# Two of three contraction parts of the context projections by Strassen's seven products, in a perceiver block on one core

## Chip, core and metric

The kernel runs on one core of a Trainium2 chip. It is timed as the device microseconds of one execution; the time before is the median of three runs, 1639.78 us (1639.32 to 1644.37). Everything is float32. The engines are TensorE (PE, matmuls; its weight loads are shown as PEld), VectorE (DVE), ScalarE (ACT), GpSimd (POOL) and SyncE (SP), which here issues all transfers. Each has its own in-order queue; they wait for each other through semaphores.

## What is computed

A block of three layers: cross attention of 32 batches of 64 tokens (width 512) to a context of 512 tokens (width 384), self attention with rotary angles, and a feed-forward layer for the better half of the tokens. Each is added to x. Cut to what the change touches:

```python
# x: (32, 64, 512); ctx_768: (32, 512, 384); the mask is all true
def _L0_xattn_ref(x, context, context_mask, Wq, Wk, Wv, Wo):      # 16 heads of 32
    q = (x @ Wq)...          # Wq: (512, 512)
    k = (context @ Wk)...    # Wk, Wv: (384, 512)
    v = (context @ Wv)...
    scores = einsum('bhid,bhjd->bhij', q, k) * scale
    attn = softmax(where(context_mask, scores, max_neg), axis=-1)
    out = einsum('bhij,bhjd->bhid', attn, v)
    return out.reshape(B, N, 512) @ Wo
...
x = x + _L0_xattn_ref(_layernorm(x), ctx_768, mask_BxS2_bf1, ...)
x = x + _L0_attn_ref(_layernorm(x), ...)
x = x + _L0_ffn_ref(_layernorm(x), ...)
```

Per batch, keys and values are two products of (512 x 384) by (384 x 512): the largest piece of arithmetic in the block.

## The kernel before, in words

**Stages.** Stage A is the cross attention, stage B the self attention, then comes the feed-forward layer. Stage A is one loop over 66 steps s (line 519); b = s // 2 is the batch and cp = s % 2 says which half of its heads is worked on. One step is called a half here.

**One half, in PE's order.** PE's instructions stand in the order in which the program writes them (`tc.manual_schedule`, line 135). The other engines' orders are made by a scheduler. A half does this:

- `score_burst` (line 188): scores of the half's 8 heads into four PSUM banks sc0 to sc3, 16 records.
- `attend` and `weighted` (lines 232, 501): the weighted sums of the half that was scored two halves ago, into bank po.
- `softmax_a` (line 203): for each of the four banks a reduction on DVE (line 208, writes sm and the minimum mn), the exponential on ACT (line 214, writes pr and its sum), the reciprocal on DVE (line 216), and on POOL the scaling of pr (line 217).
- Four rounds r = 0 to 3. Each has `flip` (line 221: four PE transposes of one pr tile of the half before into the bank pt, and a copy out of it, on DVE for even r, on ACT for odd r) and one `kv_piece` (line 145) for the next batch: in a cp = 0 half the four pieces of the keys, in a cp = 1 half the four pieces of the values. A piece is three matmuls of 512 columns, one for each 128 of the contraction of 384, into a bank "mm", and one copy to SBUF (ACT for keys, DVE for values).
- In every fourth half, `project` (line 246) in round 1: the output projection of a tile of 128 tokens, the addition to x and the statistics of the next layer norm. In cp = 0 halves, as long as a group of four tiles is still to come, round 3 ends with a piece of the next queries (`query_tile` or `query_chunk`).

**Banks.** PSUM has eight: mm twice, pt once, po once, sc0 to sc3. A bank with one buffer is written again only when its reader is done.

**Transfers.** `load_ctx(b)` brings the transposed context (768 KB) and the mask row of batch b into buffers of which there are two; it is called with `kv_start` (line 137) one batch ahead, at the beginning of a cp = 0 half. `kv_start` makes the mask tile mb on POOL. The weights of stage B (awq, awk, awv, awo) are loaded at the start, behind x (lines 130 to 133, awq first).

**The end of stage A.** In the last batch there is no next batch to project; stage B's first tiles (`early`) take the place of the pieces. From there on nothing of the change is in the program, apart from the place of three weight tiles.

Of the kernel before, what the change touches and what calls it, by code (L numbers as in the profile page):

```python
# [7 lines left out]
F32 = mybir.dt.float32  # L8
U8 = mybir.dt.uint8
AF = mybir.ActivationFunctionType  # L10
ALU = mybir.AluOpType
# [3 lines left out]
P = 128  # L15
NB, S, D = 32, 64, 512
M, DC = 512, 384
# [5 lines left out]
NCC = DC // P  # L23
# [17 lines left out]
def perceiver_block(  # L41
# [3 lines left out]
    nc = tc.nc  # L45
# [4 lines left out]
    wbpool = ctx.enter_context(tc.tile_pool(name="wb", bufs=1))  # L50
# [4 lines left out]
    def chunked(w):  # L55
        return w.rearrange("(c p) f -> p c f", p=P)

    def load(pool, w, tag):
        k, f = w.shape
        t = pool.tile([P, k // P, f], F32, tag=tag, name=tag)  # L60
        nc.sync.dma_start(t, chunked(w))
        return t

    def row2k(tag, bufs, name, shape=(P, D)):
        return work.tile(list(shape), F32, tag=tag, name=name, bufs=bufs)
# [3 lines left out]
    def bank(tag, name, shape=(P, 512)):  # L69
        return ps.tile(list(shape), F32, tag=tag, name=name, bufs=2 if tag == "mm" else 1)  # L70
# [33 lines left out]
    wa = only_a.enter_context(tc.tile_pool(name="wa", bufs=1, side="right"))  # L104
    kvp = only_a.enter_context(tc.tile_pool(name="kv", bufs=2, side="right"))

    def load_ctx(b):
        t = kvp.tile([P, NCC, M], F32, tag="ctxT", name=f"ctxT{b}")
        nc.sync.dma_start(t, chunked(ctxT[b]))
        m8 = kvp.tile([P, M], U8, tag="m8", name=f"m8_{b}")  # L110
        nc.sync.dma_start(m8, mask[b : b + 1, :].to_broadcast([P, M]))
        return t, m8
# [6 lines left out]
    wk = load(wa, xWk, "xWk")  # L119
    ctx0 = load_ctx(0)  # L120
    wv = load(wa, xWv, "xWv")
# [6 lines left out]
    wo = load(wa, xWo, "xWo")  # L128
    xs += [load_x(t) for t in range(GT, NT)]
    awq = load(wbpool, aWq, "aWq")  # L130
    awk = load(wbpool, aWk, "aWk")
    awv = load(wbpool, aWv, "aWv")
    awo = load(wbpool, aWo, "aWo")

    tc_order = ctx.enter_context(tc.manual_schedule(engines={mybir.EngineType.PE}))

    def kv_start(b, loaded):
        cT, m8 = loaded
        mb = kvp.tile([P, M], F32, tag="mb", name=f"mb{b}")
        nc.gpsimd.tensor_scalar(mb, m8, -BIG, BIG, ALU.mult, ALU.add)  # L140
        kT = kvp.tile([P, NC, M], F32, tag="kT", name=f"kT{b}")
        v = kvp.tile([P, NKC, D], F32, tag="v", name=f"v{b}")
        return dict(b=b, cT=cT, mb=mb, kT=kT, v=v)

    def kv_piece(kv, n):

        p = bank("mm", f"kv{kv['b']}_{n}")
        i = n % 4
        cols = slice(i * P, (i + 1) * P)
        for d in range(NCC):  # L150
            if n < 4:
                lhsT, rhs = wk[:, d, cols], kv["cT"][:, d, :]
            else:
                lhsT, rhs = kv["cT"][:, d, cols], wv[:, d, :]
            nc.tensor.matmul(p, lhsT, rhs, start=(d == 0), stop=(d == NCC - 1))  # L155
        if n < 4:
            nc.scalar.copy(kv["kT"][:, i, :], p)  # L157
        else:
            nc.vector.tensor_copy(kv["v"][:, i, :], p)  # L159

    def query_group(g):

        for t in range(g * GT, (g + 1) * GT):
            ln_stats(0, t)
        ln_rstd(0, g * GT, GT)
        return dict(
            g=g, xnT=work.tile([P, NC, GT * P], F32, tag="xnT", name=f"xnT_a{g}"),
            qT=work.tile([P, NC, GT * P], F32, tag="qT", name=f"qT_a{g}", bufs=2),
        )
# [33 lines left out]
    def softmax_a(kv, pss, cp):  # L203
        b, prs = kv["b"], []
        for r in range(4):
            sm = row2k("sm", NSM, f"sm{b}_{cp}_{r}")
            mn = small.tile([P, 1], F32, tag="mn", name=f"mn{b}_{cp}_{r}")
            nc.vector.tensor_tensor_reduce(  # L208
                out=sm, in0=pss[r], in1=kv["mb"], scale=1.0, scalar=3.4e38,
                op0=ALU.add, op1=ALU.min, accum_out=mn,  # L210
            )
            pr = row2k("pr", NPR, f"pr{b}_{cp}_{r}")
            su = small.tile([P, 1], F32, tag="su", name=f"su{b}_{cp}_{r}")
            nc.scalar.activation(pr, sm, AF.Exp, bias=mn, scale=-1.0, accum_out=su)  # L214
            ri = small.tile([P, 1], F32, tag="ri", name=f"ri{b}_{cp}_{r}")
            nc.vector.reciprocal(ri, su)  # L216
            nc.gpsimd.tensor_scalar(pr, pr, ri, None, ALU.mult)  # L217
            prs.append(pr)
        return prs

# [215 lines left out]
    def tile_steps(t):  # L436


        live = {}

        def last(n):
            return t - n if 0 <= t - n < NT else None

        here, back, done = last(0), last(1), last(2)
        ahead = t + 1 if t + 1 < NT else None
        if here is not None:
            heads_first(here, 0)
            heads_first(here, 1)
            yield 0.9
        if back is not None:  # L450
            pTs = [flip_b(back, 0, probs[back][0])]
        if ahead is not None:
            norm_b(ahead)
        if back is not None:
            pTs.append(flip_b(back, 1, probs[back][1]))
        yield 1.3
        if here is not None:
            probs[here] = [softmax_b(here, 0)]
        if done is not None:
            live = choose(done)  # L460
        if ahead is not None:
            roped(project_b(ahead, awq, "q"), 0)
            yield 4.1
        if back is not None:
            oT = weighted_b(back, pTs)
        if here is not None:
            probs[here].append(softmax_b(here, 1))
        yield 2.0
        if ahead is not None:
            roped(project_b(ahead, awk, "k"), 1)  # L470
            yield 3.4
        if back is not None:
            project_y(back, oT)
            yield 3.4
        if done is not None:
            gather(done, *live)
        if ahead is not None:
            nc.scalar.copy(slot("xv", 2 + ahead % 2), project_b(ahead, awv, "v"))
            yield 3.4
# [3 lines left out]
    def stage_b(first, last):  # L483
        for t in range(first, last):
            yield from tile_steps(t)


    kv = kv_start(0, ctx0)
    for n in range(8):
        kv_piece(kv, n)  # L490
    group = query_group(0)
    for j in range(GT):
        query_tile(group, j)
    for c in range(NC):
        query_chunk(group, c)
    nxt = kv_start(1, ctx1)

    halves = []
# [18 lines left out]
    ready = None  # L517
    early = None
    for s in range(2 * NB + 2):
        b, cp = s // 2, s % 2  # L520
        if b < NB:
            if s and cp == 0:
                kv = nxt
                nxt = kv_start(b + 1, load_ctx(b + 1)) if b + 1 < NB else None
            pss = score_burst(kv, group["qT"], cp)
        if s >= 2:
            ready = attend()
        flips = halves[0] if halves else None
        if b < NB:
            half = dict(id=f"{b}_{cp}", kv=kv, cp=cp, pTs=[])  # L530
            half["prs"] = softmax_a(kv, pss, cp)
            halves.append(half)
        g, at = divmod(b, 2 * GT)
        if s == 2 * GT * 2 * g and g + 1 < NT // GT and b < NB:
            coming = query_group(g + 1)
        if b < NB and nxt is None and early is None:
            buf["xv"] = work.tile([P, 4, D], F32, tag="xnT", name="xv_b")
            buf["rope"] = work.tile([P, 4, D], F32, tag="wq", name="rope_b")
            buf["qk"] = work.tile([P, 4, D], F32, tag="qT", name="qk_b", bufs=2)
            early = stage_b(-1, 2)  # L540
        more = b < NB and g + 1 < NT // GT
        for r in range(4):
            if flips is not None:
                flip(flips, r)
            if b < NB and nxt is not None:
                kv_piece(nxt, 4 * cp + r)
            elif early is not None:
                spent = 0.0
                while spent < 2.2:
                    took = next(early, None)  # L550
                    if took is None:
                        break
                    spent += took
            if ready is not None and r == 1:
                project(*ready)
                ready = None
            if more and cp == 0 and r == 3:
                if at < GT:
                    query_tile(coming, at)
                else:  # L560
                    query_chunk(coming, at - GT)
        if more and at == 2 * GT - 1 and cp:
            group = coming
# [79 lines left out]
    for fc in range(NFC):  # L643
        tag, bufs = W2_HOME[fc]
# [80 lines left out]
```

## Time and profile before

| | us |
|---|---|
| median of three runs | 1639.78 |
| the profiled execution | 1639.23 |
| its span, first to last instruction | 1637.4 |
| from the start to the first score burst | 47.93 |
| from there to the first score burst of the last batch (62 halves) | 986.62 |
| the last batch's two halves and what follows, to 1110 us | 75.45 |
| stage B's rest and the feed-forward layer | 527.40 |

A half without `project` and without a query piece lasts 14.37 us (1002.39 to 1016.76). In it DVE runs for 3.7 us of reductions, four reciprocals and two flip copies, ACT four exponentials of 0.72 us with 0.19 us to read their sums, POOL four scalings of 1.55 us.

How to read the lines: a group's row has the source line, engine, operation, output <- inputs by the program's names, the shape, the count, then busy us and mean ns of one, and the idle time of the engine just ahead of these instructions with what ended it. A matmul's duration holds its pipeline's fill and drain, so that records that follow each other overlap; what one costs in a stream is the distance from one start to the next. A float32 matmul shows as two records. A row of a timeline has the start, the duration, and in brackets the idle time before it.

### The profile page before, as it was taken

What the parts mean: (1) busy time and instruction counts of PE and PEld (TensorE: products, weight loads), DVE (VectorE), ACT (ScalarE), POOL (GpSimd) and SP (SyncE); (2) the same over time, 40 slices, a digit from 0 to 9 for tenths busy, and PEclk for the clock granted to TensorE, in tenths of its full rate; (3) what the DMA queues carried; (4) which work ended last, traced back from release to release, by engine and by line L of the source; (5) the groups of instructions that cost most, each with busy time, mean ns of one, the idle gap of its engine ahead of it and who ended that gap; (6) DMA issues with size and microseconds to landing.
All of it is one profiled execution on the core that took longest, in us unless ns stands there. A gap on an engine that the chain in (4) does not pass through costs nothing. (4 is left out here: it accounts for less than half of the span.)

```text
span 1637.4 us, 28162 instructions
## 1 busy us (share of the span) xinstructions
PE 1599.7 (98%) x11584; PEld 800.8 (49%) x11584; DVE 683.3 (42%) x1725; ACT 456.5 (28%) x1012; POOL 549.0 (34%) x440
## 2 busy tenths in 40 slices
PE   7999999999999999999999999889999998999998
PEld 3455444554444454544444454445555555444443
DVE  3333434443434343434343343447777777101001
ACT  1343332333323333333233333221222222210100
POOL 0434343434433434434344444433333333000000
PEclk9999999999999999999999999999999999999999
DMA  9100100010001000100010010002000002001001
GB/s 348 41 22 23 42 22 22 24 41 22 23 23 41 22 22 24 41 22 22 23 41 22 23 46 1 1 3 109 1 1 2 1 8 74 24 0 39 13 13 39
DMA packets 29520, 54.58 MB, mean 33 GB/s; under 512 B 2128, under 2 KB 6224, under 8 KB 28880
## 3 DMA queue, kind: packets, MB, share of 16 engines
q1 hardware_dynamic: 29392, 52.77, 9.8%
q8 instruction: 92, 1.51, 0.4%
q14 instruction: 36, 0.29, 0.1%
HBM read 48.57 MB, written 4.19 MB: 32 GB/s over the span
## 5 line engine op out<-in xcount | busy, mean ns | idle before, releaser
L217 POOL TENSOR_SCALAR pr<-pr,ri 128x512 f32<-128x512 f32 x256 | 396.4, 1563 | 535.7 <-DVE ri L216 529.5
L155 PE MATMUL kv<-ctxT,xWk 128*128 128x512 f32 x768 | 351.9, 596 | 7.7 <-DMA ctxT<-in_ctxT 7.7
L155 PE MATMUL kv<-xWv,ctxT 128*128 128x512 f32 x768 | 350.3, 593 | 0.0
L214 ACT ACTIVATE pr<-sm,mn 128x512 f32<-128x512 f32 x256 | 183.7, 718 | 285.6 <-DVE mn L208 220.5
L208 DVE CUSTOM_DVE_ANT_0 sm<-sc,mb 128x512 f32<-128x512 f32 x256 | 171.7, 689 | 87.7 <-PE sc L197 87.7
L155 PEld LDWEIGHTS kv<-ctxT,xWk 128*128 128x128 f32 x768 | 137.2, 191 | 135.0 <-issue 133.9
L155 PEld LDWEIGHTS kv<-xWv,ctxT 128*128 128x128 f32 x768 | 136.2, 190 | 124.3 <-issue 124.1
L101 PEld LDWEIGHTS pt<-cst,pr 128*128 128x128 f32 x1024 | 117.7, 141 | 125.3 <-issue 73.3
L101 PE MATMUL pt<-cst,pr 128*128 128x128 f32 x1024 | 158.9, 278 | 6.6 <-DVE rope_b L288 3.1
L159 DVE COPY v<-kv 128x512 f32<-128x512 f32 x128 | 88.4, 691 | 159.7 <-PE kv L155 159.5
L157 ACT COPY kT<-kv 128x512 f32<-128x512 f32 x128 | 74.8, 585 | 205.9 <-PE kv L155 205.9
L227 ACT COPY pT<-pt 128x512 f32<-128x512 f32 x128 | 73.8, 577 | 203.4 <-PE pt L101 203.4
L611 PE MATMUL ups<-W,hT 128*128 128x512 f32 x256 | 111.8, 595 | 0.0
L229 DVE COPY pT<-pt 128x512 f32<-128x512 f32 x128 | 87.7, 685 | 56.5 <-PE pt L101 56.5
L599 PE MATMUL hps<-selT,W 128*128 128x512 f32 x256 | 110.7, 593 | 0.0
L216 DVE RECIPROCAL ri<-su 128x1 f32<-128x1 f32 x256 | 40.8, 159 | 109.0 <-ACT pr L214 95.4
L338 POOL TENSOR_TENSOR pr_b<-pr_b,ri_b 128x512 f32<-128x512 f32 x32 | 33.4, 1043 | 155.5 <-DVE ri_b L337 146.1
L240 PEld LDWEIGHTS po<-pT,v 128*32 128x32 f32 x4096 | 60.1, 110 | 51.2 <-issue 51.2
L618 DVE TENSOR_TENSOR up<-ups,b_bc 128x512 f32<-128x512 f32 x8 | 5.5, 691 | 176.6 <-PE ups L611 176.6
L611 PEld LDWEIGHTS ups<-W,hT 128*128 128x128 f32 x256 | 48.1, 190 | 62.9 <-issue 62.9
L599 PEld LDWEIGHTS hps<-selT,W 128*128 128x128 f32 x256 | 48.4, 190 | 60.5 <-issue 60.5
L197 PE MATMUL sc<-kT,qT_a 32*64 32x512 f32 x1024 | 71.3, 613 | 0.0
(94 smaller groups left out, 1484.1 us busy)
## 6 DMA issues: line engine op xcount, KB each, us to landing
ctxT<-in_ctxT SPq DMA_DIRECT2D x32, 768.0 KB, 4.8
x<-in_x SPq DMA_DIRECT2D x16, 256.0 KB, 8.9
W<-in_W SPq DMA_DIRECT2D x1, 4096.0 KB, 12.6
W<-in_W SPq DMA_DIRECT2D x16, 256.0 KB, 3.2
out<-o SPq DMA_DIRECT2D x16, 256.0 KB, 2.0
m<-in_mask SPq DMA_DIRECT2D x32, 64.0 KB, 2.8
wq<-in_xWq SPq DMA_DIRECT2D x1, 1024.0 KB, 10.1
xWo<-in_xWo SPq DMA_DIRECT2D x1, 1024.0 KB, 10.4
```

The source lines that it names most:

```text
L101: nc.tensor.transpose(into[:, c, :], src[:, c * P : (c + 1) * P], ident)
L155: nc.tensor.matmul(p, lhsT, rhs, start=(d == 0), stop=(d == NCC - 1))
L157: nc.scalar.copy(kv["kT"][:, i, :], p)
L159: nc.vector.tensor_copy(kv["v"][:, i, :], p)
L197: nc.tensor.matmul(pss[r][S * i : S * (i + 1), :], qT[rows, 2 * cp + i, at : at + S], kv["kT"][rows, 2 * cp + i, :], start=True, stop=True,)
L208: nc.vector.tensor_tensor_reduce(out=sm, in0=pss[r], in1=kv["mb"], scale=1.0, scalar=3.4e38, op0=ALU.add, op1=ALU.min, accum_out=mn,)
L214: nc.scalar.activation(pr, sm, AF.Exp, bias=mn, scale=-1.0, accum_out=su)
L217: nc.gpsimd.tensor_scalar(pr, pr, ri, None, ALU.mult)
L227: nc.scalar.copy(pT, p)
L229: nc.vector.tensor_copy(pT, p)
L599: nc.tensor.matmul(p, w1[:, d, fc * P : (fc + 1) * P], late["selT"][n][:, d, :], start=(d == 0), stop=(d == NC - 1),)
L611: nc.tensor.matmul(p, hTs[n, fc // 4][:, fc % 4, j * P : (j + 1) * P], w2[fc], start=(fc == 0), stop=(fc == NFC - 1),)
```

## The change

Keys and values are each a product with a contraction of 384 = 3 x 128. For the first two parts of 128, the product of a 2 x 2 grid of blocks by a 2 x 2 grid of blocks is made by Strassen's seven products in place of eight; the blocks are 128 (contraction) by 256. The third part keeps its number of columns, as eight matmuls of 256; its terms are accumulated into the banks of the seven products ("lo" and "hi" with "both", "first" or "second", where "both" is the sum of the two halves of the context and serves two of the four result blocks together).

- `weight_sums` makes, once, five sums or differences of weight blocks and one negation, for Wk on DVE and for Wv on POOL.
- `kv_start` makes, for each batch, three DVE instructions of sums and differences of context blocks into cs (512, 256 and 768 elements a partition).
- `kv_steps` is a generator of seven steps for each of keys and values. Its matmuls have 256 columns; steps 1 to 3 have two each and open the banks pb, pa and pc, and each bank is copied out by ACT and then, in steps 4 to 6, accumulated into further, without being cleared. Steps 4 to 7 have four matmuls each. ACT makes five copies, POOL four additions or subtractions in SBUF, DVE two additions of a bank to an SBUF block.
- pc lies in the bank sc0, the fourth bank "d" again in "mm".
- In the four rounds of a half, rounds 0 to 2 take two steps and round 3 takes one. `project` moves from round 1 to the end of round 3 in the halves that have such steps.
- `kv_start` and `load_ctx` are called a half earlier, for batch b + 2, at cp = 1.
- The tiles of awk, awv and awo are used for the sums until the last batch; the three loads move from the start to there.
- The scaling of pr gets a second operation (times 1.0).

```diff
-    awk = load(wbpool, aWk, "aWk")
-    awv = load(wbpool, aWv, "aWv")
-    awo = load(wbpool, aWo, "aWo")
...
+    HALFW = M // 2
+    spare = wbpool.tile([P, 8 * HALFW], F32, tag="aWk", name="spare")
+    wkx = spare[:, 0 : 3 * HALFW].rearrange("p (i f) -> p i f", i=3)
+    held = spare[:, 3 * HALFW : 7 * HALFW].rearrange("p (i f) -> p i f", i=2)
+    wvx = wa.tile([P, 3, HALFW], F32, tag="wvx", name="wvx")
+
+    def weight_sums(w, x, engine):
+        a11, a21 = w[:, 0, 0:HALFW], w[:, 0, HALFW:M]
+        a12, a22 = w[:, 1, 0:HALFW], w[:, 1, HALFW:M]
+        engine.tensor_tensor(x[:, 0, :], a11, a22, ALU.add)
+        engine.tensor_tensor(x[:, 1, :], a21, a22, ALU.add)
+        engine.tensor_tensor(x[:, 2, :], a11, a12, ALU.add)
+        engine.tensor_tensor(a21, a21, a11, ALU.subtract)
+        engine.tensor_tensor(a12, a12, a22, ALU.subtract)
+        engine.tensor_scalar(a11, a11, -1.0, 1.0, ALU.mult, ALU.mult)
...
+    wks = weight_sums(wk, wkx, nc.vector)
+    wvs = weight_sums(wv, wvx, nc.gpsimd)
 
     def kv_start(b, loaded):
         cT, m8 = loaded
+        cs = wbpool.tile([P, 6, HALFW], F32, tag=("aWv", "aWo")[b % 2], name=f"cs{b}")
+        nc.vector.tensor_tensor(
+            cs[:, 3:5, :].rearrange("p i k -> p (i k)"), cT[:, 1, :], cT[:, 0, :], ALU.subtract
+        )
+        nc.vector.tensor_tensor(cs[:, 5, :], cT[:, 0, 0:HALFW], cT[:, 1, HALFW:M], ALU.add)
+        nc.vector.tensor_tensor(
+            cs[:, 0:3, :], cT[:, :, 0:HALFW], cT[:, :, HALFW:M], ALU.add
+        )
...
-    def kv_piece(kv, n):
...
+    def kv_steps(kv, part):
+        w, c, b = (wks, wvs)[part], kv["c"], kv["b"]
+
+        def product(p, wn, cn, start=False, stop=False):
+            for j in range(2):
+                cols = slice(j * P, (j + 1) * P)
+                lhsT, rhs = (c[cn][:, cols], w[wn]) if part else (w[wn][:, cols], c[cn])
+                nc.tensor.matmul(
+                    p[:, j, :], lhsT, rhs, start=start and j == 0, stop=stop,
+                    skip_group_check=True,
+                )
...
+        pb = open_bank("mm", "b")
+        product(pb, "m3", "m3", start=True)
+        nc.scalar.copy(c11, pb)
+        yield
+        pa = open_bank("mm", "a")
+        product(pa, "m4", "m4", start=True)
+        nc.scalar.copy(c22, pa)
+        yield
+        pc = open_bank("sc0", "c")
+        product(pc, "m1", "m1", start=True)
+        nc.scalar.copy(x1, pc)
+        nc.gpsimd.tensor_tensor(c11, c11, c22, ALU.add)
+        nc.gpsimd.tensor_tensor(c22, c11, x1, ALU.add)
+        yield
+        product(pb, "m5", "m5")
+        product(pb, "lo", "second", stop=True)
+        nc.scalar.copy(c12, pb)
+        nc.gpsimd.tensor_tensor(c11, c11, c12, ALU.subtract)
+        yield
+        product(pa, "m2", "m2")
+        product(pa, "hi", "first", stop=True)
+        nc.scalar.copy(c21, pa)
+        nc.gpsimd.tensor_tensor(c22, c22, c21, ALU.subtract)
+        yield
+        product(pc, "m7", "m7")
+        product(pc, "lo", "both", stop=True)
+        nc.vector.tensor_tensor(c11, pc, c11, ALU.add)
+        yield
+        pd = open_bank("mm", "d")
+        product(pd, "m6", "m6", start=True)
+        product(pd, "hi", "both", stop=True)
+        nc.vector.tensor_tensor(c22, pd, c22, ALU.add)
+        yield
...
-            nc.gpsimd.tensor_scalar(pr, pr, ri, None, ALU.mult)
+            nc.gpsimd.tensor_scalar(pr, pr, ri, 1.0, ALU.mult, ALU.mult)
...
             if s and cp == 0:
-                kv = nxt
-                nxt = kv_start(b + 1, load_ctx(b + 1)) if b + 1 < NB else None
+                kv, nxt = nxt, after
...
             halves.append(half)
+            if cp:
+                after = kv_start(b + 2, load_ctx(b + 2)) if b + 2 < NB else None
+            if nxt is not None:
+                steps = kv_steps(nxt, cp)
...
+            awk = load(wbpool, aWk, "aWk")
+            awv = load(wbpool, aWv, "aWv")
+            awo = load(wbpool, aWo, "aWo")
             early = stage_b(-1, 2)
...
             if b < NB and nxt is not None:
-                kv_piece(nxt, 4 * cp + r)
+                next(steps)
+                if r < 3:
+                    next(steps)
...
-            if ready is not None and r == 1:
+            if ready is not None and r == (3 if b < NB and nxt is not None else 1):
                 project(*ready)
                 ready = None
```

More of the change, by code (lines that the diff above doesn't have):

```diff
@@ L130, in perceiver_block @@
     awq = load(wbpool, aWq, "aWq")
-    awk = load(wbpool, aWk, "aWk")
-    awv = load(wbpool, aWv, "aWv")
-    awo = load(wbpool, aWo, "aWo")
     tc_order = ctx.enter_context(tc.manual_schedule(engines={mybir.EngineType.PE}))
+    HALFW = M // 2
[12 more added lines that the diff above has]
+        engine.tensor_scalar(a11, a11, -1.0, 1.0, ALU.mult, ALU.mult)
+        return {
+            "m1": x[:, 0, :], "m2": x[:, 1, :], "m3": a11, "m4": a22, "m5": x[:, 2, :],
+            "m6": a21, "m7": a12, "lo": w[:, 2, 0:HALFW], "hi": w[:, 2, HALFW:M],
+        }
+    wks = weight_sums(wk, wkx, nc.vector)
+    wvs = weight_sums(wv, wvx, nc.gpsimd)
     def kv_start(b, loaded):
         cT, m8 = loaded
+        cs = wbpool.tile([P, 6, HALFW], F32, tag=("aWv", "aWo")[b % 2], name=f"cs{b}")
[6 more added lines that the diff above has]
+        )
         mb = kvp.tile([P, M], F32, tag="mb", name=f"mb{b}")
@@ L142, in kv_start @@
         v = kvp.tile([P, NKC, D], F32, tag="v", name=f"v{b}")
-        return dict(b=b, cT=cT, mb=mb, kT=kT, v=v)
-    def kv_piece(kv, n):
[L147 to L159, printed above, removed]
+        c = {
+            "m1": cs[:, 5, :], "m2": cT[:, 0, 0:HALFW], "m3": cs[:, 4, :], "m4": cs[:, 3, :],
+            "m5": cT[:, 1, HALFW:M], "m6": cs[:, 0, :], "m7": cs[:, 1, :],
+            "first": cT[:, 2, 0:HALFW], "second": cT[:, 2, HALFW:M], "both": cs[:, 2, :],
+        }
@@ new lines, in kv_start, with home, open_bank @@
+        return dict(b=b, c=c, mb=mb, kT=kT, v=v)
+    def kv_steps(kv, part):
[8 more added lines that the diff above has]
+                )
+        def home(f, k):
+            if part:
+                return kv["v"][:, 2 * k : 2 * k + 2, f * HALFW : (f + 1) * HALFW]
+            return kv["kT"][:, 2 * f : 2 * f + 2, k * HALFW : (k + 1) * HALFW]
+        def open_bank(tag, n):
+            return bank(tag, f"kv{b}_{part}_{n}", (P, 2, HALFW))
+        c11, c12, c21, c22 = home(0, 0), home(0, 1), home(1, 0), home(1, 1)
+        x1 = held[:, part, :].rearrange("p (j k) -> p j k", j=2)
+        pb = open_bank("mm", "b")
[31 more added lines that the diff above has]
+        yield
@@ L488, in perceiver_block @@
     kv = kv_start(0, ctx0)
-    for n in range(8):
-        kv_piece(kv, n)
+    for part in range(2):
+        for _ in kv_steps(kv, part):
+            pass
     group = query_group(0)
```

## The prediction

> **What bounds the kernel now.** I read the page first, then the same engines by stretch, then one period in order of time.
>
> ```profile
> PE 1599.7 (98%) x11584; PEld 800.8 (49%) x11584; DVE 683.3 (42%) x1725; ACT 456.5 (28%) x1012; POOL 549.0 (34%) x440
> ...
> L155 PE MATMUL kv<-ctxT,xWk 128*128 128x512 f32 x768 | 351.9, 596 | 7.7 <-DMA ctxT<-in_ctxT 7.7
> L155 PE MATMUL kv<-xWv,ctxT 128*128 128x512 f32 x768 | 350.3, 593 | 0.0
> ...
> L101 PE MATMUL pt<-cst,pr 128*128 128x128 f32 x1024 | 158.9, 278 | 6.6 <-DVE rope_b L288 3.1
> ```
>
> TensorE (PE) is busy 98% of the span. The projection that is changed, L155, is 1536 of its records: 32 batches x 2 parts x 12 matmuls, each matmul shown as two records. The transposes of line 101 lost 6.6 us in all, so the vector engines are never felt. By stretches of time, the steady part of stage A is full:
>
> ```profile
> 47.93:1034.55 986.62, 984.68 (x7561) 485.86 (x7560) 396.90 (x1092) 342.34 (x784) 411.44 (x295) 1.00 0.09 26
> ```
>
> Columns: length, then busy time of PE, PEld, DVE, ACT, POOL, then the granted clock (1.00). In 986.62 us PE is busy 984.68. That says that PE work removed is time removed, but only until another engine stands just behind. So I look at one half-batch ("half") in order of time, PE and then VectorE (DVE):
>
> ```profile
> 1002.39 1.11 PE L197 MATMUL sc<-kT,qT_a 32*64 32x512 f32 x16
> 1003.44 1.10 PE L240 MATMUL po<-pT,v 128*32 128x64 f32 x64
> 1004.47 0.66 PE L101 MATMUL pt<-cst,pr 128*128 128x128 f32 x4
> 1004.96 2.74 PE L155 MATMUL kv<-ctxT,xWk 128*128 128x512 f32 x6
> 1007.59 0.63 PE L101 MATMUL pt<-cst,pr 128*128 128x128 f32 x4
> ...
> 1016.76 1.11 PE L197 MATMUL sc<-kT,qT_a 32*64 32x512 f32 x16
> ```
>
> ```profile
> 1002.50 0.69 DVE L159 COPY v<-kv 128x512 f32<-128x512 f32 x1 [2.33 <-PE kv L155]
> 1003.57 0.69 DVE L208 CUSTOM_DVE_ANT_0 sm<-sc,mb 128x512 f32<-128x512 f32 x1 [0.37 <-PE sc L197]
> 1004.18 0.69 DVE L208 CUSTOM_DVE_ANT_0 sm<-sc,mb 128x512 f32<-128x512 f32 x1
> ...
> 1005.30 0.16 DVE L216 RECIPROCAL ri<-su 128x1 f32<-128x1 f32 x1 [0.42 <-ACT pr L214]
> 1005.44 0.69 DVE L208 CUSTOM_DVE_ANT_0 sm<-sc,mb 128x512 f32<-128x512 f32 x1
> ...
> 1006.14 0.69 DVE L208 CUSTOM_DVE_ANT_0 sm<-sc,mb 128x512 f32<-128x512 f32 x1
> ...
> 1006.76 0.69 DVE L229 COPY pT<-pt 128x512 f32<-128x512 f32 x1
> ```
>
> Measure all from the score burst (1002.39 = 0). The half lasts 14.37. The first flip starts at 2.08, the first projection piece at 2.57, the second flip at 5.20. There is one "pt" bank, so the second flip must wait until DVE has copied the first flip out. That copy stands behind four softmax reductions in DVE's queue, runs from 4.37 and ends at 5.06. **The margin before DVE holds PE is 5.20 - 5.06 = 0.14 us.** That is the number on which this change turns.
>
> **The change part by part.**
>
> *Matmul columns.* Per part 12 matmuls of 512 columns become 22 of 256: 24 records to 44. Price: six 512-column records and the flip behind them repeat every 3.01-3.02 us (601.62 to 604.63 elsewhere in the timeline); four 128-column records take 0.44 of it, so a 512-column one takes 0.429 and a 128-column one 0.107 to 0.11. No record has 256 columns. From below, in proportion: 0.2145. From above, the 64-column records of L428, the nearest ordinary matmuls with full weights (eight in 1.00 us, 0.125 each): the line from there to 0.429 gives 0.255. I take 0.2145, because the 128-column records lie on the proportional line. The weight loads last 0.19 and fit under it. So 24 x 0.429 - 44 x 0.2145 = 0.86 us less PE work per half, 64 x 0.86 = 55 us in all.
>
> [...]
>
> *Where the columns go.* Between the first and the second flip stood one piece, 6 x 512 = 3072 columns. Now the first two steps stand there, 8 records x 256 = 2048. Behind the second flip stood 18 x 512; now 12 + 16 + 8 = 36 records x 256, the same 9216. **The whole saving lies ahead of the second flip.** It would start at 2.57 + 8 x 0.2145 + 0.05 (the seam seen before) = 4.34, but DVE's order in the built program is unchanged there (four reductions, then the copy), so the copy ends at 5.06 and the flip starts at about 5.15. The rest keeps its 14.37 - 5.20 = 9.17. The half becomes 14.32: of 0.86 us, 0.81 turns into a wait and 0.05 is gained. Over 62 halves: -3 us.
>
> *Context sums.* kv_start adds three DVE instructions per batch (512, 256 and 768 elements). Two SBUF operands on DVE: L329, 512 elements, 0.68 us, next start 0.60 later; 256 elements fewer are 0.27 less (L322 with 256: 0.415; L252 with 512: 0.691), so 0.33, 0.60 and 0.87 for the three. Sum 1.80. They are queued behind the v part's last addition, which waits for PE's last step, and ahead of the next half's reductions. Today the copy in that place starts at 0.11 (1002.50) and the first reduction at 1.18. Then: addition 0.11-0.72, sums to 2.53, first reduction 2.53. It is 1.35 late, the whole chain to the second flip with it, and PE waits as much again. Cover for this exists only where a projection of the output (L249, 3.4 us) ends the half. In the built order 15 halves have the sums bare: 15 x 1.35 = +20.
>
> *Output projection moved from the second to the last place.* There its DVE tail now comes just ahead of the reductions. In a half at 645 us: addition 0.20 after its last matmul, statistics 0.6 to 0.72 later, aggregate +0.72, variance +0.22, then the reduction: 0.20 + 0.72 + 0.72 + 0.22 + 0.12 = 1.98 against 1.18, 0.8 late; earlier it lay under the next projection piece. 13 halves: +10. Two more have four further tiles' statistics there, some 4 x 0.7: 2 x 3.6 = +7.
>
> *ScalarE* now takes five copies of 0.58 per half in place of two on average; with four exponentials (0.72 + 0.19) and two flip copies that is 7.7 of 14.3 us. Each product that reopens a bank waits for such a copy; the tightest is step four, whose copy ends near 5.3 while step four is reached at 6.4. Nothing on the path; without that cover it would be 0.58 per half.
>
> *GpSimd (POOL).* Four additions per half, and pr's scaling gets a second operation.
>
> ```profile
> L217 POOL TENSOR_SCALAR pr<-pr,ri 128x512 f32<-128x512 f32 x256 | 396.4, 1563 | 535.7 <-DVE ri L216 529.5
> L338 POOL TENSOR_TENSOR pr_b<-pr_b,ri_b 128x512 f32<-128x512 f32 x32 | 33.4, 1043 | 155.5 <-DVE ri_b L337 146.1
> L402 POOL TENSOR_TENSOR x<-x,hid 128x512 f32<-128x512 f32 x16 | 27.4, 1712 | 18.8 <-DVE hid L95 18.8
> L140 POOL TENSOR_SCALAR mb<-m 128x512 f32<-128x512 uint8 x32 | 19.8, 618 | 11.3 <-DMA m<-in_mask 11.3
> ```
>
> An addition costs 1.04 (L338) to 1.28 (the first L402, whose DVE neighbours have one SBUF operand). The scaling lies between 0.62 (L140, two operations, constants, a byte input) and 1.56 (L217, today's). With 0.62 to 1.1 the chain of additions is done before the last step ends near 14.3, and costs nothing; that cover is the step itself. With 1.56 and 1.28 it runs: scalings one to three from 3.23 to 7.9, additions and the last scaling on to 14.5, or 15.1 where the mask row (0.62) comes too: 0.9 late in the 15 bare halves, +14. I take the two-operation row, +0, and keep +14 for the range.
>
> L402 mostly takes 1.78, 0.50 more, when a DVE instruction with two SBUF operands (L398) starts with it; L329 is such an instruction and lies between 0.68 and 0.85. The context sums have two SBUF operands too, but they follow a DVE addition that waits for GpSimd's last one, so I add nothing; one such meeting per batch, 30 x 0.50, would be +15, and goes into the range. [...]
>
> *Start and loads.* DVE's sums of Wk (six of 256 at 0.33, 2.0) and the first of context 0 (0.60) precede the first matmul, which started at 7.7: 0.6 late if Wk landed early, 2.6 at most; the first batch saves 1.7. Taken: 0. The loads of awk, awv, awo move from 26 us in SP's queue, where nothing waited for them, to the end of stage A; awk may start once the spare tile is free, about 9 us into half 61, and is first needed about 10 us later. 768 KB take 4.8 us. Nothing; uncovered, one such load each.
>
> **Sum.** -3 + 20 + 10 + 7 = +34 on the profiled 1639.23 us (span 1637.4, the rest around it unchanged), 0.5 below the median 1639.78: **1674 us**.
>
> **Rivals.** (a) GpSimd late, as priced: 1674 + 14 = 1688. For it, the unexplained 1.56; against it, four adds and four scalings make 11.7 of 14.3 us. Chance 0.20. (b) The second flip is not held: the copy out of the first flip ends by 4.34 instead of 5.06, and the sums lie in a gap. Then all comes through: 1639 - 53 = 1586. It decides if DVE's chain loses 0.8 us of its 3.9; only the 0.42 wait for the exponential is slack there. Chance 0.08. (c) The flip is held, but sums and tail find cover: about 1637. Chance 0.05; the queue order speaks against it. (d) The 256-column record costs 0.255: 36 of the 44 are not in the stall, 36 x 0.04 x 62 = +90, less what covers the sums: near 1750. Chance 0.05. My forecast: 0.62.
>
> **Numbers.** 0.3% of 1640 is 5 us, what a measurement can tell from no change. Faster: (b), and little of (c): 0.09. Same: 0.06. Slower: 0.85. The range goes from 1648 (sums half hidden) to 1700 ((a) with most of the 15 us of meetings): 1648-1700.
>
> **What would show it.** Right: idle time on PE ahead of pt, released by DVE's pT copy, some 50 us at the shorter waits and twice that with the late halves; kv records near 0.215 apart; first reductions 2.5 us after the burst in every fourth half. Wrong: pt idle under 10 us, or idle time ahead of sc released by the addition into sc0's half (GpSimd late), or 256-column records above 0.23.

## The result, and the profile after

The changed kernel takes 1692.34 us (median of 4 runs, 1687.84 to 1694.7) where the kernel before took 1639.81 beside it: a ratio of 1.0309, 95% interval 1.029 to 1.0328. The profiled execution took 1691.83, its span 1690.0. The forecast, 1674, had the sign and the mechanism; of the 52.6 us that the span grew it had 34.

The page of the kernel after, its first line and two groups (busy us, mean ns | idle before, releaser):

```profile
PE 1576.5 (93%) x12864; PEld 1058.1 (63%) x12864; DVE 749.8 (44%) x1827; ACT 553.8 (33%) x1204; POOL 655.5 (39%) x702
...
L293 POOL TENSOR_SCALAR pr<-pr,ri 128x512 f32<-128x512 f32 x256 | 177.2, 693 | 376.6 <-DVE ri L292 308.6
...
L101 PE MATMUL pt<-cst,pr 128*128 128x128 f32 x1024 | 161.0, 280 | 79.3 <-DVE ri L292 74.7
```

PE's share fell from 98% to 93%: it does less and waits. The line of the flips, which had lost 6.6 us, now loses 79.3, of which 74.7 in 60 waits ended by DVE (columns: us in total, times, the longest):

```profile
PE pt L101 <- DVE ri L292: 74.7, 60, 3.2
```

(The view names the reciprocal L292, the last DVE instruction to signal; it stands right behind the copy of the first flip out of "pt", L305.) By stretches, first the same 62 halves as before, then 65 us out of them; columns as before:

```profile
51.48:1083.24 1031.76, 957.01 (x8801) 732.05 (x8800) 452.13 (x1176) 436.08 (x970) 509.93 (x542) 0.99 0.09 28
...
780.00:845.00 65.00, 60.97 (x486) 45.31 (x484) 25.38 (x63) 23.94 (x53) 29.91 (x31) 0.97 0.09 27
```

The 62 halves last 1031.76 in place of 986.62, +45.1. The start grew by 3.6 (first score burst at 51.48, before 47.93), the part behind half 62 by 3.9 (606.8, before 602.85). And there is something that the steady part of the kernel before did not have: a granted clock of TensorE below 1.00, here 0.97.

PE by the timeline, one half with the context sums ahead of it (988.40) and one without (1036.86):

```profile
988.40 1.11 PE L273 MATMUL sc<-kT,qT_a 32*64 32x512 f32 x16
...
994.92 0.63 PE L101 MATMUL pt<-cst,pr 128*128 128x128 f32 x4 [2.06 <-DVE ri L292]
...
1036.86 1.11 PE L273 MATMUL sc<-kT,qT_a 32*64 32x512 f32 x16
...
1039.43 1.03 PE L188 MATMUL kv_b<-xWv,cs 128*128 128x256 f32 x4
1040.30 1.03 PE L188 MATMUL kv_a<-xWv,cs 128*128 128x256 f32 x4
1041.97 0.63 PE L101 MATMUL pt<-cst,pr 128*128 128x128 f32 x4 [0.65 <-DVE ri L292]
1042.43 1.03 PE L188 MATMUL kv_c<-wvx,cs 128*128 128x256 f32 x4
...
1051.18 0.69 PE L273 MATMUL sc<-kT,qT_a 32*64 32x512 f32 x8
```

The plain half lasts 1051.18 - 1036.86 = 14.32, against 14.37 before: seven products, and 0.05 us to show for them. Its second flip starts 5.11 after the burst (before: 5.20), held by "pt". In the half with the sums it starts 6.52 after the burst. DVE says why:

```profile
988.58 0.69 DVE L234 TENSOR_TENSOR v<-kv_d,v 128x512 f32<-128x512 f32 x1 [1.47 <-PE kv_d L188]
989.19 0.68 DVE L161 TENSOR_TENSOR cs<-ctxT 128x512 f32<-128x512 f32 x1
989.78 0.42 DVE L164 TENSOR_TENSOR cs<-ctxT 128x256 f32<-128x256 f32 x1
990.12 0.95 DVE L165 TENSOR_TENSOR cs<-ctxT 128x768 f32<-128x768 f32 x1
990.99 0.68 DVE L284 CUSTOM_DVE_ANT_0 sm<-sc,mb 128x512 f32<-128x512 f32 x1
...
994.08 0.69 DVE L305 COPY pT<-pt 128x512 f32<-128x512 f32 x1
```

Last addition, three sums, and only then the first reduction, 2.59 after the burst (forecast 2.53). The copy that frees "pt" starts at 994.08, 5.68 after the burst, where it started at 4.37 before.

**The missing part: the clock.** The first such half with a late load, in PE's order:

```profile
173.63 1.03 PE L188 MATMUL kv_a<-cs,xWk 128*128 128x256 f32 x4
177.72 1.09 PE L101 MATMUL pt<-cst,pr 128*128 128x128 f32 x4 [3.06 <-DVE ri L292]
178.60 1.92 PE L188 MATMUL kv_c<-cs,spare 128*128 128x256 f32 x4
180.31 1.21 PE L188 MATMUL kv_b<-ctxT,spare 128*128 128x256 f32 x4
181.35 1.03 PE L188 MATMUL kv_b<-ctxT,xWk 128*128 128x256 f32 x4
```

After the wait the four 256-column records take 1.71 to the next start, twice the 0.87 of the plain half, and 3 us later all is as usual. From 177.72 to 181.00 the granted clock averages 0.55 (the third number from the end):

```profile
177.72:181.00 3.28, 3.28 (x11) 2.85 (x12) 0.16 (x1) 2.17 (x5) 2.61 (x3) 0.55 0.00 0
```

The clock records of the trace show nine such stretches at half speed (a granted clock of 0.50) in the 62 halves, each 3.413 us long; the kernel before has none there. Every one begins near the end of a wait of at least 2.06 us (from 0.5 us before it to 1.1 us behind it), and none stands at a wait of 1.87 or less.

**A ledger.** Half by half, the time after minus the time before is the half's waits less some 0.70 us of work, and in the nine halves with a half-speed stretch some 1.65 more. Sorted, in us:

| | forecast | measured |
|---|---|---|
| plain saving, all 62 halves | -3 | -4.0 |
| 15 halves with bare sums: wait beyond 0.65 | +20 | +23.9 |
| the same halves: half-speed clock | not in the sum | +14.9 |
| 12 halves with the tail of project | +10 (13 of them) | +9.2 |
| 2 halves with four tiles' statistics too | +7 | +0.7 |
| one more half | - | +0.3 |
| start | 0 | +3.6 |
| behind half 62 | 0 | +3.9 |
| sum | +34 | +52.5 |

### The profile page after: what moved, and what is told of

Read it like the earlier page. It is cut to its first block, busy times and chain, and to the rows that moved or that the text cites. A ratio compares the mean times of both kernels' runs of the same rounds, so it can differ in the third digit from the quotient of the medians.

```text
span 1690.0 us, 31285 instructions
## 1 busy us (share of the span) xinstructions
PE 1576.5 (93%) x12864; PEld 1058.1 (63%) x12864; DVE 749.8 (44%) x1827; ACT 553.8 (33%) x1204; POOL 655.5 (39%) x702
## 5 line engine op out<-in xcount | busy, mean ns | idle before, releaser
L293 POOL TENSOR_SCALAR pr<-pr,ri 128x512 f32<-128x512 f32 x256 | 177.2, 693 | 376.6 <-DVE ri L292 308.6
L101 PE MATMUL pt<-cst,pr 128*128 128x128 f32 x1024 | 161.0, 280 | 79.3 <-DVE ri L292 74.7
L284 DVE CUSTOM_DVE_ANT_0 sm<-sc,mb 128x512 f32<-128x512 f32 x256 | 171.5, 689 | 13.5 <-PE sc L273 12.9
L305 DVE COPY pT<-pt 128x512 f32<-128x512 f32 x128 | 88.1, 688 | 124.8 <-PE pt L101 124.8
L292 DVE RECIPROCAL ri<-su 128x1 f32<-128x1 f32 x256 | 40.9, 160 | 126.5 <-ACT pr L290 126.3
L92 POOL TENSOR_TENSOR rstd<-var,mhalf 128x1 f32<-128x1 f32 (+1 forms) x36 | 22.1, 615 | 150.5 <-DVE var L91 150.2
L316 PE MATMUL po<-pT,v 128*32 128x64 f32 x4096 | 70.4, 220 | 0.0
L688 ACT ACTIVATE hT<-hps,b_sb 128x512 f32<-128x512 f32 x32 | 22.0, 687 | 146.1 <-PE hps L684 146.1
L355 PE MATMUL q_b<-aWq,xv_b 128*128 128x512 f32 x128 | 61.1, 622 | 2.6 <-ACT xv_b L349 2.6
L229 DVE TENSOR_TENSOR v<-kv_c,v 128x512 f32<-128x512 f32 x32 | 22.1, 692 | 91.5 <-PE kv_c L188 85.5
L229 DVE TENSOR_TENSOR kT<-kv_c,kT 128x512 f32<-128x512 f32 x32 | 22.1, 691 | 89.7 <-PE kv_c L188 79.4
```

The costliest lines, as they stand in the source:

```text
L101: nc.tensor.transpose(into[:, c, :], src[:, c * P : (c + 1) * P], ident)
L284: nc.vector.tensor_tensor_reduce(out=sm, in0=pss[r], in1=kv["mb"], scale=1.0, scalar=3.4e38, op0=ALU.add, op1=ALU.min, accum_out=mn,)
L293: nc.gpsimd.tensor_scalar(pr, pr, ri, 1.0, ALU.mult, ALU.mult)
L305: nc.vector.tensor_copy(pT, p)
L316: nc.tensor.matmul(po[32 * r : 32 * r + 32, c, :], v[:, k, HD * h : HD * (h + 1)], half["pTs"][r][:, k, S * i : S * (i + 1)], start=(k == ...
L355: nc.tensor.matmul(p, xnT[:, d, :], w[:, d, :], start=(d == 0), stop=(d == NC - 1))
```

## The experiments

Each was timed against the kernel before on its chip (1639.39 to 1641.21 us); ratios are to that kernel, with their 95% intervals.

### Fewer columns in the kernel before, ahead of the flip or behind it

The prediction's main step says that a saving ahead of the second flip turns into a wait. The kernel before can show it without Strassen: the third contraction part (two records of 512 columns, 0.86 us) is left out, once in the first piece, ahead of the second flip, and once in the third.

```diff
-        for d in range(NCC):
+        for d in range(NCC - (i == 0 and kv["b"] > 0)):     # other run: i == 2
...
-            nc.tensor.matmul(p, lhsT, rhs, start=(d == 0), stop=(d == NCC - 1))
+            nc.tensor.matmul(p, lhsT, rhs, start=(d == 0), stop=(d == NCC - 1 - (i == 0 and kv["b"] > 0)))
```

> The kernel before, with the last of the three contraction parts left out of the first piece of each half (batches 1 to 31): two records of 512 columns, 0.858 us per half, less TensorE work ahead of the second flip, 53 us in all; this is the very place from which the change took its columns, without any of its sums, copies or additions. Theory (VectorE's copy out of the first flip stood 0.14 us behind TensorE there already before the change): nearly all of it becomes waiting, the second flip comes at 5.11 in place of 5.20, 62 x 0.09 = 6 us: 1632 to 1637 us. Rival (TensorE is what bounds the stage): 1586 us.

> The control to the run with less work in the first piece: the kernel before, with the last contraction part left out of the third piece of each half, behind the third flip, the same 53 us of TensorE work. Theory: no copy stands just behind TensorE there, so it all comes through: 1585 to 1590 us. If it too stays above 1620, the limit is not at the second flip but one of throughput, and the theory falls.

Measured: 1640.8 us (0.9988, 0.9977 to 0.9998) and 1587.92 us (0.9674, 0.9655 to 0.9693). The same work, left out of two different pieces: the one is worth about 2 us (at most 4 by its interval), the other 53. PE and then DVE in the first of the two, by the timeline:

```profile
1001.00 1.11 PE L197 MATMUL sc<-kT,qT_a 32*64 32x512 f32 x16
...
1003.57 1.88 PE L155 MATMUL kv<-ctxT,xWk 128*128 128x512 f32 x4
1006.21 0.63 PE L101 MATMUL pt<-cst,pr 128*128 128x128 f32 x4 [0.75 <-DVE ri L216]
```

```profile
1005.37 0.69 DVE L229 COPY pT<-pt 128x512 f32<-128x512 f32 x1
```

The flip stands at 5.21, where it stood with all the work (5.20), and the half lasts 14.37 as before. I had expected 3 to 8 us of gain from the margin of 0.14; even that did not come through. The copy ends at 1006.06 and the flip, which now waits for it, starts 0.15 later. So the 0.14 of the kernel before was about the time from a copy's end to the flip that it releases, and there was no slack. Rival (b) falls with this.

### The steps placed otherwise

In the changed kernel, steps 1 and 2 stand ahead of the second flip. One more step there gives PE 0.87 us of work while DVE's chain runs, with the same total.

```diff
-                next(steps)
-                if r < 3:
-                    next(steps)
+                for _ in range((3, 1, 1, 2)[r]):
+                    next(steps)
```

> The changed kernel with the seven steps spread over the rounds as 3, 1, 1, 2 in place of 2, 2, 2, 1, so that 12 records of 256 columns (3072 columns, as before the change) stand ahead of the second flip. Theory (the saved columns were taken from ahead of the second flip, where VectorE's copy of the first flip is the limit): every wait ahead of the second flip shrinks by up to 4 x 0.216 = 0.865 us, the 0.65 us waits vanish, 74.7 us of waits become about 27, and with no wait above 2 us outside the late transfers the clock stays up: 1630 to 1642 us. Rival 1 (the smaller, more numerous matmuls with their weight loads are what costs): nothing changes, 1692. Rival 2 (GpSimd's and ScalarE's added work is the limit): new waits of the same size ahead of the third or fourth flip or the scores, 1680 to 1700.

Measured: 1631.2 us (0.9941, 0.9924 to 0.9959), 61 us below the changed kernel. PE's waits:

```profile
PE pt L101 <- DVE ri L292: 27.5, 29, 2.1
```

The waits of the plain halves are gone, those of the halves with sums fall to 1.2 us, those behind project to 0.45. Two half-speed stretches are left in the 62 halves, both behind waits of 2.05 us.

### The context sums on GpSimd

```diff
-        nc.vector.tensor_tensor(            # all three into cs
+        nc.gpsimd.tensor_tensor(
```

> The changed kernel with the three context sums of a batch on GpSimd in place of VectorE. Theory: the waits of 2.06 us and more (15 halves) fall to 0.65, about 15 x 1.4 + 5 = 26 us, the half-speed clock windows behind them go too (9 in stage A, about 1.5 us each): 1650 to 1660 us. Rival (GpSimd's added work is the limit): 3.9 us more on GpSimd per batch make it slower, above 1700. If only the waits count and not the clock: about 1666.

Measured: 1647.95 us (1.0047, 1.0032 to 1.0062), 2 us below the expected range.

```profile
PE pt L101 <- DVE ri L292: 49.2, 59, 1.8
```

45 waits are now of 0.65 us and 11 of 1.32, the plain price and that of project, none above 1.8, and no stretch at half speed is left in the 62 halves. So the three sums on DVE cost 44 us of the 52, where the prediction's term has 20: the waits that they make are 25.5 us of it (74.7 - 49.2), the clock that follows them 14.9, and the rest lies ahead of the 62 halves (first burst at 50.0) and behind them.

### Project back in round 1

```diff
-            if ready is not None and r == (3 if b < NB and nxt is not None else 1):
+            if ready is not None and r == 1:
```

> The changed kernel with the output projection back in round 1. Theory by the trace: the projection at the end of a half covers the context sums, so putting it back lays them bare in 13 to 15 more halves: waits of 1.32 become 2.06, +0.74 x 14 = +10 us, and about half of these waits drop the clock (+1.5 us each, +10): 1700 to 1715 us. Rival (as the prediction priced it, the move costs 0.8 us each time and putting it back is a gain): 1675 to 1685.

Measured: 1711.12 us (1.0437, 1.0405 to 1.047).

```profile
PE pt L101 <- DVE ri L292: 84.9, 60, 3.5
PE y_a L325 <- ACT v L219: 10.1, 15, 0.7
```

Undoing the move makes it slower. The move has two sides: DVE's tail behind project costs 9.9 us in 14 halves, but while PE is at project, the sums of the next batch run unseen. Without it the waits of 2.05 us and more go from 15 to 29, and project itself meets a bank that ACT has not copied yet, 0.68 us in 15 halves. The rival, that the moved project costs as much as forecast and no more hangs on it, falls.

### One product twice: is the clock a cause of its own?

Step 2's product is issued twice into the cleared bank (the second clears it again). It adds four records, 0.87 us, to every half, in the place where PE waits, so that the waits become short without a change in DVE's order.

```diff
         product(pa, "m4", "m4", start=True)
+        product(pa, "m4", "m4", start=True)
```

> The changed kernel with the product of step 2 issued twice: four more records of 256 columns (0.865 us) per half, standing just ahead of the second flip, 64 x 0.865 = 55 us more TensorE work. Theory (TensorE only waits there, and long waits drop the clock): plain halves lose 0.865 - 0.65 = 0.2 us each, 31 x 0.2 = +7, the longer waits swallow it whole, and as waits shrink from 2.06 to 1.2 us the half-speed windows vanish, -12: 1683 to 1692 us. Without the effect on the clock: 1699. Rival (TensorE is the limit): 1747.

Measured: 1679.87 us (1.0242, 1.0214 to 1.027), below the expected 1683 to 1692: with 55 us more work for PE, it takes 12 us less than the changed kernel. If a wait cost only its own length, filling it would change nothing in the halves that waited at least 0.87 and lengthen the others. Waits, and the stretch that had 0.97 above:

```profile
PE pt L101 <- DVE ri L293: 30.9, 29, 2.6
```

```profile
780.00:845.00 65.00, 63.35 (x576) 47.24 (x575) 28.43 (x75) 26.76 (x60) 29.25 (x33) 1.00 0.07 24
```

The waits of 2.06 became 1.19, the clock is 1.00 again, and no half-speed stretch is left in the 62 halves. Half by half against the changed kernel, the nine halves that had a half-speed stretch lose 13.8 us in all, the 21 others that had waited 0.87 or more change by 0.7, and the 32 left grow by 1.8. That a wait of 2 us can cost more than 2 us, through the clock, is shown by this run. The gain came out larger than expected because the plain halves grew by 0.02 each in place of 0.2: the idle time of 0.65 is counted from the end of the last record ahead of it, and four such records show 1.03 us where they repeat every 0.865, so that nearly the whole 0.865 fitted in. Four waits of 2.1 to 2.6 us stay in this run without such a stretch, so that a part of the 13.8 may be how the waits fell (see the last section).

### The scaling with one operation again

Rival (a) was a late GpSimd. The change gives pr's scaling a second operation, times 1.0, which looks like nothing. It was taken away from the changed kernel, and put alone into the kernel before.

```diff
-            nc.gpsimd.tensor_scalar(pr, pr, ri, 1.0, ALU.mult, ALU.mult)
+            nc.gpsimd.tensor_scalar(pr, pr, ri, None, ALU.mult)
```

> The changed kernel with pr's scaling as one operation again (times ri, no second operation), as in the kernel before. It tests rival (a) of the prediction, GpSimd late: with scalings of 1.56 us and additions of 1.27 us the chain of additions should end late. GpSimd has then 4 x 1.56 + 4 x 1.27 = 11.3 us of work in halves of 15 to 16.6 us. If the second operation is what keeps GpSimd in time, the scalings are back at 1.56 us, the last VectorE addition waits for GpSimd, idle time ahead of sc or pt grows, and the time is 1700 to 1712 us (the 14 us of the rival and some more half-speed windows). If it doesn't matter, because the halves have become longer than the 14.3 us that the rival was priced for, the time stays at 1688 to 1695.

> The kernel before with the second operation (times 1.0) in pr's scaling, and nothing else of the change. The scalings should last 0.69 us in place of 1.56. GpSimd was on nothing's path there, so the time should be that of the kernel before, 1637 to 1643 us; if the scaling's length set anything, or if a faster GpSimd met VectorE more often, it moves by more than 3 us.

Measured: 1700.83 us (1.0364, 1.0341 to 1.0386) and 1641.4 us (1.0006, 0.9994 to 1.0019). The scaling by its line in the two (duration ns min/median/max), first in the changed kernel with one operation:

```profile
L293 POOL TENSOR_SCALAR pr<-pr,ri x256: 1552/1562/1572, 54.8 to 1127.8; 128x512 f32<-128x512 f32 x128
```

and in the kernel before with two:

```profile
L217 POOL TENSOR_SCALAR pr<-pr,ri x256: 688/692/908, 51.8 to 1069.0; 128x512 f32<-128x512 f32 x128
```

With 1.56 us the last DVE additions wait for GpSimd (16.0 us in 30 waits and 13.5 in 23; in the changed kernel 1.6 in 3), and PE's waits show what rival (a) foresaw, the score burst held by the addition into sc0's half:

```profile
PE sc L273 <- DVE v L229: 3.5, 12, 1.2
```

So the rival's mechanism is real and worth 8.5 us, not 14, and the second operation is what kept it away. In the kernel before, where GpSimd is on no path, the same operation makes no difference.

### Steps and sums together, and project in round 2

The two edits that helped, in one kernel; then the same with project in round 2, where the tail of its statistics lies between two projection pieces again.

```diff
-            if ready is not None and r == (3 if b < NB and nxt is not None else 1):
+            if ready is not None and r == (2 if b < NB and nxt is not None else 1):
```

> The changed kernel with both moves: steps spread 3, 1, 1, 2 and the context sums on GpSimd. Theory: stage A's records and seams without waits take 942 us in the run with the sums on GpSimd (992.2 - 49.9); left are waits of 0.45 in the 13 halves behind an output projection and about 1 in two more, 8 us; with 50 us of start and 604 us of what follows: 1604 to 1610 us. If the two moves do not add (another limit stands close by): 1620 or more.

> As the run with both moves, and the output projection in round 2, behind the third flip's step and ahead of the fourth flip, so that its addition and statistics on VectorE do not stand ahead of the reductions. Theory: the last 8 us of waits go: 1597 to 1603 us. Rival (the projection's bank waits for a copy, as it did in round 1, 0.68 us in 15 halves): 1608 to 1615.

Measured: 1604.33 us (0.977, 0.9753 to 0.9787) and 1602.54 us (0.9759, 0.9744 to 0.9773). Both beat both kernels; the second is the best version found, though the two can't be told apart by their intervals. Its time is in the expected range, but its theory, that the last waits go, is not what its profile shows: the waits of about 0.45 behind the projection are gone, while others grew, two of 2.16 and one of 2.05 us among them, with two half-speed stretches (the granted clock is 0.99 over its 62 halves, 1.00 in the first). In the 62 halves PE waits 8.3 us in place of 9.6. The 62 halves of the first:

```profile
49.79:996.48 946.69, 936.61 (x8801) 717.42 (x8800) 399.94 (x1089) 424.46 (x970) 617.32 (x629) 1.00 0.09 30
```

PE is busy 98.9% of them at full clock, GpSimd 65%. The seven products do save time: these halves last 39.9 us less than in the kernel before, once the saved columns no longer stand ahead of a wait and the sums no longer ahead of the reductions.

## Why the prediction was right, and where it was too small

The measured 1692.34 lies inside the stated range, but partly by luck. The room above 1674 had been put there for a late GpSimd (14 us) and for meetings of GpSimd and VectorE (15 us). Neither happened in the changed kernel; the clock and late transfers, which the sum did not have, filled the same room. That 1692 is near rival (a)'s 1688 is chance too.

**The place of the saving: right.** That all of it lies ahead of the second flip and only 0.05 of 0.86 us comes through was the step on which the sign hung; the half is 14.32 as forecast, and the two runs on the kernel before show it by itself. The margin of 0.14 was in truth nothing.

**The 256-column record: taken a little low.** Four of them repeat every 0.865 us (1039.43 to 1040.30, 1042.43 to 1043.30), 0.2163 each against 0.2145 taken. So 44 x 0.0018 = 0.08 less is saved per half. The 8 records ahead of the second flip only shorten the wait (0.65 by the view for 0.81; the view counts four records as 1.03 us busy where they repeat every 0.865, which is the difference). The 36 behind it cost 0.06 of time: from the second flip on the half lasts 9.21 where 9.17 was taken. The flip came at 5.11 where 5.15 was taken, so that the two small errors cancel in the 14.32. Rival (d) is out.

**The sums, 15 x 1.35 = 20: the mechanism right, the size wrong. This is the step that failed.** The wait itself was 2.06 where 2.16 was expected. Two things were left out. (1) The price of a wait was taken as its length. At nine of these 15 waits TensorE then ran for 3.413 us at half clock (0.50 granted), which cost 14.9 us together. (2) In the built order the sums of a batch stand in DVE's queue behind the load whose buffer has just come free; the first of them waits for it 10 times, 7.6 us in all, with the reductions queued behind. In the half at 170 us the load lands about 171.9 and the first sum starts at 171.98, with 0.92 us of waiting, so that its PE wait is 3.06. Five of the 15 waits are longer than 2.06, by 2.7 us in all, most of the 3.9 between 20 and 23.9. The prediction read the queue order for the sums' place, not for what they themselves wait for.

**Project, +10 and +7: the one right, the other wrong.** The tail costs 0.66 in most halves where 0.8 was taken. The two halves with four tiles' statistics already waited 0.88 us in the kernel before, so little was added. And the prediction counted only what the move costs; the run that undoes it is 19 us slower.

**Start: 0 taken, +3.6 measured.** The first batch's kv_a waits 2.1 us for DVE's addition, with one half-speed stretch at 23.6 to 27.0 us. The other runs with the same start code have 1.9 to 3.9.

**The end: 0 taken, +3.9 measured, and not the change's for certain.** The profiled execution of the kernel before with the second operation, 1644.01 us, has 606.7 us behind half 62, with two half-speed stretches within 85 us of it; its other executions cluster at 1639 and 1644, and so do those of the kernel before. The run with steps and sums together, whose program is the changed kernel's there, has 603.2 us and no such stretch in these 85 us. So the program itself costs some 0.3 us there and the clock most of the rest. How often each kernel meets such a stretch there was not counted.

**ScalarE, the weight loads and the meetings of GpSimd and VectorE: taken at nothing, and nothing came.** No wait of PE on ScalarE's copies is among those of the 62 halves. The weight loads of the 256-column records last 0.19 us each, less than the 0.216 from record to record. The meetings did not happen: in 31 of the 32 batches GpSimd ran nothing while the three sums ran (in the half at 988.40 it is idle from 986.55 to 992.98). So the 15 us kept in the range for them were not needed, but what a meeting would cost is not shown. The 0.50 that the prediction read for one was GpSimd's side alone: in the kernel before, VectorE's copy L405, behind L398, lasts 1.18 us from 1129.39, beside GpSimd's L402 (1128.70 to 1130.48), and 0.22 at 1112.43, where L402 had ended at 1110.67.

Rival (c) was that the sums and the tail find cover. The run with project moved back shows it in part: cover exists in the halves that end with project, as the sum had it; the 15 halves with bare sums had none.

## What to carry to other kernels

Before removing work from the engine that is busy 98% of the time, measure how long the next engine's copy or bank release stands behind it at that very place: here work saved there was worth next to nothing, and the same work saved two pieces later was worth all of it (2 and 53 us). When a wait on TensorE can't be avoided, keep it short or fill it; waits of 2 us and more were often paid for again in clock here (nine of 15, some 1.65 us each). And read what a moved instruction waits for itself, because the queue behind it waits too: here the first sum waited 0.92 us for its load in the half at 170 us, and the reductions with it.

## What the hardware showed

**Behind waits of 2 us TensorE's granted clock fell to 0.50.** In the changed kernel the stretches at 0.50 last 3.413 us each (one of them twice that), and their starts lie whole multiples of that apart (from 23.65 to 177.25 us 45 of them). With a grid of that period laid through them, the ten waits between 60 and 1130 us with 2.06 us or more inside one period are followed by a half-speed stretch in the next, and no wait with less, up to 1.9, is; six waits of 2.06 that straddle two periods are followed by none. Two other runs (project back, one operation) divide at 1.9 to 2.0 us when their grid is fitted in the same way, with one fitted shift per run. All of TensorE's idle time in each period, added up, divides at the same places (2.056 us and more in the ten, up to 1.883 in the others). But the length of the wait does not decide alone: behind 1130 us a stretch begins at 1163.70 with only this wait in the period ahead of it:

```profile
1163.32 0.33 PE L483 MATMUL row<-cst,four 128*128 128x128 f32 x1 [1.58 <-DVE four L481]
```

Why 1.58 us sufficed at this place, and why the same wait is not followed by a stretch in the kernel before, stays open.

Where the grid falls may also be why runs of one kernel differ by several microseconds. Two profiles of the kernel before, of 1639.23 us and, with the second operation, of 1644.01, have the same wait behind half 62:

```profile
1039.75 3.70 PE L279 MATMUL q_b<-aWq,xv_b 128*128 128x512 f32 x8 [2.03 <-ACT xv_b L273]
```

```profile
1040.69 5.40 PE L279 MATMUL q_b<-aWq,xv_b 128*128 128x512 f32 x8 [2.03 <-ACT xv_b L273]
```

In the first it straddles two periods, with 1.41 us in the one, and no stretch follows. In the second the eight records behind it last 1.70 us longer, as much as one half-speed stretch adds (half of 3.413); that the wait lies inside one period there is an estimate from this.

**The same GpSimd scaling of 128x512 takes 1.56 us with one operation and 0.69 with two** (times a per-partition scalar; with times 1.0 behind it), in both kernels. Why was not tried.
